# First stage of a four-layer conv network: sets formed by half a stack, one set of five summed on ScalarE, loads spread as three for two sets

## The chip, the cores and the metric

One core of a Trainium2 chip runs the whole program. The metric is device time in microseconds (us) of one launch. The kernel before takes 3494.92 us (median of 3 runs, 3491.64 to 3495.92).

The engines are TensorE (PE in the profile, its weight loads PEld), VectorE (DVE), ScalarE (ACT), GpSimd (POOL) and SyncE (SP). SP does nothing here but issue DMAs, in the order in which the program lists them.

## What is computed

The input x is 8 images of 384 channels of 32 x 32 pixels, fp32. Four layers follow one another, each `x = x + layer(groupnorm(x))`. The change touches the first layer alone, and of that the part up to the first q, k and v projections:

```python
def _gn(v, G=32, eps=1e-5):                 # mean and variance over 12 channels x 1024 pixels
    ...
def _dwproj(x, dw, g, b, pw):               # for each of q, k, v
    y = depthwise_conv_3x3(x, dw)           # 384 channels, padding 1
    y = gelu(_bn(y, g, b), approximate=False)   # mean and variance over batch and pixels
    return einsum('oc,bchw->bohw', pw, y)
q, k, v = (_dwproj(_gn(x), ...) for each)   # then softmax attention with 8 heads, w_out, _bn
```

The batch norm is what ties the stage together: no gelu of q can start before the depthwise convolution has run over all 8 images and its sums are known. The raw convolution results (q, k and v of 8 images, 36 MiB) [...] are written to DRAM and fetched back image by image in the attention stage.

## The kernel before

**Stacks.** The input is laid out on the host as 16 stacks of 1.5 MiB, `m = 4k + 2h + j`: image `2k + j`, half `h` of its channel groups. A stack is a tile of 128 partitions (32 row pairs of the picture, each with its two neighbour rows) by 6 slices of 512 values; the slices are `g * 3 + c`, with `g` in 0..1 a half of the stack and `c` in 0..2 the channel within a group of three. `load_tile` (L279) brings a stack in with four DMAs of 384 KB, one for each `d` (partitions `d::4`). The first four stacks go over SP and ACT, the next four over SP (L299 to L312).

**Units and sets.** The work list (L414) has 8 units `u = (k, h)`; unit u uses stacks 2u and 2u + 1. A unit has five sets in the order `y0 a1 y1 a2 v0` (unit 6 has no v set, unit 7 has the last two, `v-1 v0`), 40 sets in all, numbered n. A set is one group of matmuls on 32-row by 32- or 64-column tiles of TensorE (L574) that fills four PSUM banks:
- `y0` and `y1` make q, k and v of channel c = 0, for half g = 0 and g = 1
- `a1` and `a2` make q and k of channel c = 1 and c = 2, for both halves g
- `v0` makes v of channels 1 and 2 for both halves

So `a1`, the second set, already reads both halves of both stacks.

**After the matmuls** ScalarE copies the four banks to a tile `y` (L585; a pool of 4 tiles of 1 MiB, `ya`), VectorE takes the sums for the batch norm from `y` with four bn_stats (L591), and SP writes `y` to DRAM in four DMAs of 256 KB each, or two of 256 KB and two of 128 KB in a y set (L605). A `y` tile is free again when its writes have landed and its sums are taken.

**The group norm** of a unit, `norm(u)` (L339), is a list of ten steps: four `begin` (three bn_stats and an aggregate, L350 and L353, for each stack and half), `sums` (L366 to L379, the last on GpSimd), `spread` (L383 to L388), and four `apply` (ScalarE, L399; L397 on VectorE for the second stack of unit 0; then the two edge rows on GpSimd, L402). The table `steps` (L420) places the steps of unit u among the sets of units u - 2 and u - 1. `norm(0)` runs whole before the first set (L517).

**Order of DMAs.** All of this has one program order on every engine (a manual schedule). At set n SP gets, in this order: up to two pending loads (from n = 3 on, L534), then the four writes of the set. The pending loads are filled by unit (`LOADS`, L521): stacks 8 to 10 at unit 0, 11 and 12 at unit 1, 13 at unit 3, 14 and 15 at unit 4, and at unit 5 the raw v, k and q of image 0, fetched back in 18 DMAs of 256 KB (`fetch_raw`, L221). At the start of unit 7 (n = 34) eight small DMAs move the group norm's sums (`x_moments`, L508). GpSimd issues the loads of the weights (`load_late`, L319) at n = 0.

**The end of the stage.** Before the matmuls of n = 38 `spread_qk` (L427) gathers the q and k sums across partitions with two small matmuls (L442) and makes scale and shift (L497). After n = 38 ScalarE runs the gelu of q of image 0, after n = 39 that of k; then PE starts the projections `pq_first` (L258) and the attention stage.

Of the kernel before, what the change touches and what calls it, by code (L numbers as in the profile page):

```python
# [7 lines left out]
F32 = mybir.dt.float32  # L8
# [47 lines left out]
def tile_kernel(ctx: ExitStack, tc: tile.TileContext, i: dict, out: bass.AP):  # L56
# [210 lines left out]
    with ExitStack() as pa:  # L267
# [11 lines left out]
        def load_tile(m, queue):  # L279

            k, h, j = m // 4, m // 2 % 2, m % 2
            t = (
                image(f"xs{m}") if m in IN_IM
                else xa.tile([P, KC, N], F32, tag="xs", name=f"xs{m}")
            )
            xs_of[m] = t.rearrange("p c n -> p (c n)").rearrange("p (k n) -> p k n", n=HALF)

            def part(d):
                w = KC * N
                s = W + (0 if d in (1, 2) else W if d == 3 else -W)  # L290
                src = i["xs"][s : s + B * C * N].rearrange("(b e m n) -> b e m n", b=B, e=2, m=32)
                queue[d].dma_start(
                    out=t.rearrange("p c n -> p (c n)")[d::4],
                    in_=src[2 * k + j, 1 - d % 2, :, h * w : (h + 1) * w],
                )

            return [lambda d=d: part(d) for d in range(4)]

        for m in range(4):  # L299
            for f in load_tile(m, (nc.sync, nc.sync, nc.scalar, nc.scalar)):  # L300
                f()
# [13 lines left out]
        sels = wa.tile([P, 2, P], F32, name="sels_sb")  # L315
        isv = wa.tile([P, 7], F32, name="isv_sb")
        msk = wa.tile([P, 24], F32, name="msk_sb")
# [9 lines left out]
        xnst = wa.tile([P, B, KC, 2, 6], F32, name="xnst")  # L327
        sy = wa.tile([P, 16, NK, 6], F32, name="sy")
        sqk = wa.tile([P, KC - 1, 2, 4, NK, 6], F32, name="sqk")
        sv = wa.tile([P, 2, 4, NK, 6], F32, name="sv")  # L330
        zy = wa.tile([P, 16, 2], F32, name="zy")
        zqk = wa.tile([P, KC - 1, 8, 2], F32, name="zqk")
        zv = wa.tile([P, 8, 2], F32, name="zv")
        fqk = wa.tile([P, 2, 2, KC], F32, name="fqk")
        fv = wa.tile([P, 2, KC], F32, name="fv")
        room = wa.tile([P, 2, 160], F32, name="room")
        fs = wa.tile([P, 16], F32, name="fs")

        def norm(u):  # L339

            k, h = divmod(u, 2)
            mv = mvs[u % 2]
            turned = sa.tile([P, 2, 32], F32, tag="gp_t", name=f"gt{u}")
            rows = sa.tile([P, 2, 2, 16], F32, tag="gp_r", name=f"gr{u}")
            ss = sa.tile([P, 2, 32], F32, tag="gp_ss", name=f"gss{u}")
            small_ = sa.tile([P, 40], F32, tag="gp_s", name=f"gs{u}")

# [67 lines left out]
        for u in range(NU0):  # L415
            order = "y0 a1 y1 a2" + " v0" * (u < NU0 - 2) + " v-1 v0" * (u == NU0 - 1)
            work += [(u, w[0], int(w[1:])) for w in order.split()]
# [9 lines left out]
        def spread_qk():  # L427

            zs, nv, ng = (zy, zqk.rearrange("p c g s -> p (c g) s")), (3, 2), 16
            at = [slice(0, 96), slice(96, 160)]  # L430
            both = [
                room[:, 0, d].rearrange("p (v s g) -> p v s g", v=n, s=2)
                for d, n in zip(at, nv)
            ]
            v0 = 0
            for z, n, dst in zip(zs, nv, both):
                masked(z, n, v0, dst)
                v0 += n
            yield
            pm = big("pmove")  # L440
            for t, d in enumerate(at):
                nc.tensor.matmul(  # L442
                    pm[:, d], lhsT=sels[:, t, :], rhs=room[:, 0, d], start=True, stop=True,
                )
            got = room[:, 1, :96].rearrange("p (x g) -> p x g", g=16)
            nc.vector.tensor_tensor(
                got, pm[:, :96].rearrange("p (x g) -> p x g", g=16),
                msk[:, :16].unsqueeze(1).to_broadcast([P, 6, 16]), ALU.mult,
            )
            fy = fs[:, :6].rearrange("p (v s) -> p v s", v=3)  # L450
            nc.vector.reduce_sum(fy.rearrange("p v s -> p (v s)"), got, AX.X)
            got = room[:, 1, 96:].rearrange("p (x g) -> p x g", g=8)
            nc.vector.tensor_tensor(
                got, pm[:, 96:160].rearrange("p (x g) -> p x g", g=8),
                msk[:, 16:24].unsqueeze(1).to_broadcast([P, 8, 8]), ALU.mult,
            )
            f = fs[:, 8:16]
            nc.vector.reduce_sum(f, got, AX.X)
            nc.vector.tensor_copy(
                fqk[:, :, :, 1:], f.rearrange("p (v s c) -> p v s c", v=2, s=2)  # L460
            )
            nc.vector.tensor_copy(fqk[:, :, :, 0], fy[:, :2])
            nc.vector.tensor_copy(fv[:, :, 0], fy[:, 2])
            for v in range(2):
                scale_of(v, fqk[:, v])

        def masked(z, n, v0, dst):

            ng = z.shape[1]
            sq = sa.tile([P, ng], F32, tag="ssq", name=f"ssq{v0}")  # L470
            nc.vector.tensor_tensor(sq, z[:, :, 0], z[:, :, 0], ALU.mult)
            nc.vector.tensor_tensor(z[:, :, 1], z[:, :, 1], sq, ALU.add)
            for s in range(2):
# [5 lines left out]
        def spread_v():  # L479

            both = sa.tile([P, 32], F32, tag="bothv", name="bothv")
            masked(zv, 2, 5, both.rearrange("p (c s g) -> p c s g", c=2, s=2))
            yield
# [32 lines left out]

        for f in norm(0):  # L517
            f()
        quads = [slice(32 * r, 32 * r + 32) for r in range(4)]
        loads, norms_of = [], {}  # L520
        LOADS = {0: (8, 9, 10), 1: (11, 12), 3: (13,), 4: (14, 15)}  # L521
        for n, (u, kind, s) in enumerate(work):
            k, h = divmod(u, 2)
            at = n - first[u]
            if at == 0:
                for m in LOADS.get(u, ()):
                    loads += load_tile(m, 4 * (nc.sync,))
                if u == 0:
                    load_late()
                if u == 5:  # L530
                    acts[0] = {v: image(f"g{v}_0") for v in (2, 1, 0)}
                    for v, t in acts[0].items():
                        loads += fetch_raw(t, v, rqk[0], rv[:, 0])
            for _ in range(2):  # L534
                if loads and n > 2:
                    loads.pop(0)()
            if u == NU0 - 1 and at == 0:
# [15 lines left out]
            if kind == "v":  # L553
                h, c = h + s, 0
            else:
                c = s if kind == "a" else 0
            passes = [(j, x) for j in range(2 if kind == "v" else 1) for x in (1, 0, 2)]
            nq = 2 if kind == "y" else 4
            cols = [slice(P // nq * q, P // nq * (q + 1)) for q in range(nq)]
            for p in passes:  # L560
                j, x = p
                c0, c1 = max(0, 1 - x), W - max(0, x - 1)
                for q in range(nq):
# [3 lines left out]
                    elif kind == "y":  # L567
                        g, j, w = s, q, slice(0, 64)
                    else:
                        (g, j), w = divmod(q, 2), slice(0, 32)  # L570
                    src = xs_of[4 * k + 2 * h + j][:, g * KC + c, :]
# [11 lines left out]
            y = ya.tile([P, 4, HALF], F32, tag="y", name=f"y{n}")  # L583
            for src, r, w in outs:
                nc.scalar.copy(y[:, r : r + w, :].rearrange("p a n -> p (a n)"), src)  # L585
            st = (
                sy[:, 8 * h + 4 * s : 8 * h + 4 * s + 4] if kind == "y"
                else sv[:, h] if kind == "v" else sqk[:, s - 1, h]
            )
            for r in range(4):  # L590
                nc.vector.bn_stats(st[:, r, k, :], y[:, r, :])  # L591
            for q in range(4):
# [8 lines left out]
                else:  # L601
                    g, j = divmod(q, 2)
                    to = rqk[2 * k + j, s]
                g = 4 * (2 * h + g)
                nc.sync.dma_start(out=to[:, g : g + 4, :], in_=y[rows])  # L605
            if k == last:
                for r in range(4):
                    nc.vector.bn_aggr(
                        zy[:, 8 * h + 4 * s + r, :] if kind == "y"
                        else zv[:, 4 * h + r, :] if kind == "v" else zqk[:, s - 1, 4 * h + r, :],  # L610
                        st[:, r].rearrange("p a b -> p (a b)"),
                    )
            if n == len(work) - 2:
                gelu_image(acts[0][0], 0)
        assert not loads
        gelu_image(acts[0][1], 1)
# [1430 lines left out]
def _layouts(a):  # L2047
# [19 lines left out]
    for r in range(4):  # L2067
        for d in range(4):
# [11 lines left out]
        [  # L2080
            (own & (row % 64 < 48)).astype(f) / f(4),
            (own & (row // 64 == part // 32 % 2)).astype(f) / f(4),
# [3 lines left out]
        [  # L2086
            row // 16 % 4 == np.arange(3), row // 16 % 2 == np.arange(2),
            row // 32 % 2 == np.arange(2),
# [84 lines left out]
```

## Time and profile before

| what | value |
|---|---|
| runs of the kernel before | 3491.64, 3494.92, 3495.92 us |
| the profiled execution's own time | 3494.72 us |
| its span, first to last instruction | 3492.9 us |
| first matmul of the stage | 24.79 us after the span's start |
| first write of a `y` tile | 31.90 us |
| last write of the stage issued | 231.78 us |
| first projection `pq_first` on PE | 221.68 us |
| PE busy in the whole span | 3384.1 us (97%) |

The profile gives for each engine the time in which it was busy, and for each idle stretch what ended it (`<-ACT y` means that the instruction waited last for ScalarE's write of y). A queue's own lines (SPq) show the DMA issues: the time of an issue is how long the queue was held by it, not how long the transfer took. A table by windows shows busy time of each engine in us, the granted clock of TensorE, the mean busy share of the 16 DMA engines and the rate in GB/s. In the first 300 us the DMA engines move 78.38 MB, most of it in the first stage.

### The profile page before, as it was taken

The page shows a single profiled execution, that of the slowest core. Times are in us where ns is not written, and L with a number is a line of the kernel's source. Part 1 is how long each engine was busy: PE and PEld are TensorE (multiplying, and loading weights), DVE is VectorE, ACT ScalarE, POOL GpSimd, SP SyncE. Part 2 cuts the span into 40 slices and gives each one's busy share as a digit, 9 for nine tenths or more (in the row PEclk, how much of TensorE's full clock was granted, in tenths as well). Part 3 has the DMA queues.
Part 4 walks back from the last instruction along what each step waited for, and adds up shares of the span by engine and source line. Part 5 has one row for each costly group of instructions (what it writes and reads, how often), then busy time and mean ns, then how long its engine had stood idle before and what let it go on. Part 6 is the DMA issues. An engine that isn't in the chain of part 4 may idle for free.

```text
span 3492.9 us, 44919 instructions
## 1 busy us (share of the span) xinstructions
PE 3384.1 (97%) x18599; PEld 1458.3 (42%) x18599; DVE 1696.7 (49%) x2881; ACT 1298.5 (37%) x1514; POOL 206.1 (6%) x231
## 2 busy tenths in 40 slices
PE   6999999999999999998999999999999999999888
PEld 2333434343434343443344445344453444534434
DVE  8942232323232323234366365663656637566573
ACT  5655544444444444433222323313233232232222
POOL 2100000000000000000000200102001020010112
PEclk9999999999999999999999999999999999999898
DMA  9972121212121212123500101101111011110000
GB/s 357 295 205 79 26 79 27 79 26 79 26 79 26 79 27 78 28 79 125 220 24 21 50 39 35 40 21 50 40 35 40 21 50 40 35 39 18 0 37 19
DMA packets 86259, 234.01 MB, mean 67 GB/s; under 512 B 21672, under 2 KB 21896, under 8 KB 79130
## 3 DMA queue, kind: packets, MB, share of 16 engines
q1 hardware_dynamic: 83882, 222.75, 19.9%
q10 hardware_dynamic: 1248, 4.72, 0.3%
q8 instruction: 150, 2.46, 0.3%
q0 software_dynamic: 912, 3.53, 0.3%
q14 instruction: 67, 0.55, 0.1%
HBM read 145.77 MB, written 75.59 MB: 63 GB/s over the span
## 4 chain that ended last, share of the span: by engine, by line
PE 41%; DVE 9%; DMA 1%; ACT 1%; POOL 0%; issue 0%; DVEq 0%; ACTq 0%; POOLq 0%; SPq 0%
PE y L1502 12%; PE ph L1481 10%; DVE y L1577 5%; PE pq L1622 4%; PE pw L1585 3%; PE pf L1929 3%; PE s L1800 2%; PE pav L1826 2%; DVE hd L1467 1%; DMA o<-o 1%; PE pk L1775 1%; PE pv L1784 1%; PE xsb L1761 1%; PE pss L1839 1%; PE plog L1231 1%; DVE off L1692 1%
## 5 line engine op out<-in xcount | busy, mean ns | idle before, releaser
L827 ACT ACTIVATE p<-s 128x1024 f32<-128x1024 f32 x512 | 496.3, 1021 | 365.7 <-PE s L820 365.5
L835 PE MATMUL pav<-p,vt 64*64 64x512 f32 x4096 | 494.7, 588 | 0.0
L1481 PE MATMUL ph<-h,w_sb 128*128 128x512 f32 x1104 | 486.8, 595 | 6.3 <-ACT h L1430 6.3
L1502 PE MATMUL y<-hd,w_sb 128*128 128x512 f32 x1080 | 488.7, 600 | 3.5 <-DVE hd L1467 3.5
L820 PE MATMUL s<-qk,qk 48*64 48x512 f32 x2944 | 355.1, 592 | 0.0
L1481 PEld LDWEIGHTS ph<-h,w_sb 128*128 128x128 f32 x1104 | 207.0, 190 | 267.5 <-issue 249.8
L1502 PEld LDWEIGHTS y<-hd,w_sb 128*128 128x128 f32 x1080 | 199.9, 191 | 248.2 <-issue 235.8
L835 PEld LDWEIGHTS pav<-p,vt 64*64 64x64 f32 x4096 | 168.2, 133 | 273.7 <-issue 273.4
L796 DVE COPY ta<-pav 128x512 f32<-128x512 f32 (+1 forms) x65 | 44.2, 682 | 475.5 <-PE pav L835 475.5
L1491 ACT ACTIVATE hd<-ph,b_sb 128x512 f32<-128x512 f32 x180 | 122.7, 682 | 312.7 <-PE ph L1481 312.7
L1577 DVE SCALAR_TENSOR_TENSOR y<-h,tap,y 128x961 f32<-128x961 f32 (+1 forms) x192 | 233.8, 1241 | 0.6
L574 PE MATMUL pk<-xs,cws_sb 32*32 32x496 f32 (+3 forms) x3840 | 179.4, 601 | 39.4 <-DMA xs<-in_xs_dram 24.8
L1692 DVE SCALAR_TENSOR_TENSOR off<-q,dw_sb,off 128x225 f32<-128x225 f32 (+3 forms) x432 | 211.9, 544 | 1.6
L820 PEld LDWEIGHTS s<-qk,qk 48*64 48x64 f32 x2944 | 109.1, 133 | 211.4 <-issue 190.5
L1817 ACT ACTIVATE p<-s 128x1024 f32<-128x1024 f32 x96 | 96.1, 1023 | 166.5 <-PE s L1800 141.7
L81 DVE COPY qk<-pq 128x512 f32<-128x512 f32 x46 | 31.8, 691 | 251.9 <-PE pq L258 251.9
L1467 DVE TENSOR_TENSOR hd<-hd,cb 128x512 f32<-128x512 f32 x180 | 122.3, 684 | 41.0 <-ACT hd L1491 40.8
L574 PEld LDWEIGHTS pk<-xs,cws_sb 32*32 32x32 f32 (+1 forms) x3840 | 77.7, 111 | 139.4 <-issue 54.0
L1585 PE MATMUL pw<-y,upw 128*128 128x512 f32 x288 | 129.0, 601 | 4.9 <-DVE y L1577 4.9
L1862 POOL TENSOR_TENSOR p<-p,p 128x1024 f32<-128x1024 f32 x48 | 113.0, 2355 | 349.3 <-ACT p L1817 349.3
L820 PE MATMUL s<-ql,ql 48*64 48x512 f32 x1024 | 128.3, 592 | 0.2 <-ACT p L827 0.2
L1929 PE MATMUL pf<-att,wp_sb 128*128 128x512 f32 x288 | 127.6, 598 | 0.5 <-DVE x L1937 0.5
(326 smaller groups left out, 3718.1 us busy)
## 6 DMA issues: line engine op xcount, KB each, us to landing
rqk<-y SPq DMA_DIRECT2D x96, 256.0 KB
g<-rqk SPq DMA_DIRECT2D x96, 256.0 KB
xs<-in_xs_dram SPq DMA_DIRECT2D x56, 384.0 KB
g<-rv SPq DMA_DIRECT2D x48, 256.0 KB
xh<-in_x_dram SPq DMA_DIRECT2D x48, 256.0 KB
f<-in_x_dram SPq DMA_DIRECT2D x24, 512.0 KB
f<-o SPq DMA_DIRECT2D x24, 512.0 KB
o<-ot SPq DMA_DIRECT2D x42, 256.0 KB
```

What stands on the lines that cost most here:

```text
L574: nc.tensor.matmul(banks[r][cols[q]].rearrange("p (h w) -> p h w", w=W)[:, :, c0:c1], lhsT=cws[rs, c, 2 * h + g, x, w], rhs=src[rs, :, c0 ...
L820: nc.tensor.matmul(s[64 * k : 64 * k + 64, j * HALF : (j + 1) * HALF], lhsT=kt[r, k0 : k0 + 64], rhs=qt[r, h * HALF : (h + 1) * HALF], sta ...
L827: nc.scalar.activation(p, s, AF.Exp, scale=scale)
L835: nc.tensor.matmul(pav[k][64 * j : 64 * j + 64, :], lhsT=vts[b % 2][r, kc, 2 * hd : 2 * hd + 2, :].rearrange("p a b -> p (a b)"), rhs=p[r, ...
L1467: nc.vector.tensor_tensor(hd, hd, state["cb"], ALU.mult)
L1481: nc.tensor.matmul(ph, lhsT=w1[:, e, c, dc * P : (dc + 1) * P], rhs=state["h1"][c], start=(c == 0), stop=(c == KC - 1),)
L1502: nc.tensor.matmul(y, lhsT=w2[:, e, dc, m * P : (m + 1) * P], rhs=state[h, k], start=(k == 0), stop=(k == NE * KC - 1),)
L1577: nc.vector.scalar_tensor_tensor(d, f, tap2[:, c, t : t + 1], d, ALU.mult, ALU.add)
L1585: nc.tensor.matmul(pw[h], lhsT=upw2[:, c, m * P : (m + 1) * P], rhs=y[c][:, hs], start=(c == 0), stop=(c == KC - 1),)
L1622: nc.tensor.matmul(pq[h], lhsT=wq3[:, c, m * P : (m + 1) * P], rhs=h3[h][:, c, :], start=(c == 0), stop=(c == KC - 1),)
L1692: nc.vector.scalar_tensor_tensor(d, f, dw3[:, t : t + 1], d, ALU.mult, ALU.add)
L1929: nc.tensor.matmul(pf[:, hs], lhsT=wp3[:, pr, m * P : (m + 1) * P], rhs=att[:, pr, hs], start=(pr == 0), stop=(pr == NPAIR3 - 1),)
```

## The change

Four things are changed in the first stage; the arithmetic is otherwise the same.

1. **Halves at the start.** Stacks 0 and 1 are loaded as halves g (8 DMAs of 192 KB each instead of 4 of 384 KB), first both first halves, then both second ones. `norm(0)` is run twice, once for each half: its `sums` and `spread` run twice.
2. **Sets by half.** The order in a unit becomes `y0 a0 y1 a1 v0`: an a set now makes channels c = 1 and 2 of one half g. `y0 a0` read the first halves only. The destination of its four writes becomes channel 1 of both images, then channel 2 of both, at one half; it was both images at the first half, then at the second.
3. **ScalarE sums one set of five.** In `y1`, ScalarE does four Identity activations from PSUM to `y` and four Square activations in place in PSUM, each with an accumulated sum, and the four bn_stats on VectorE are gone.
4. **Loads at an even rate.** One load before even sets, two before odd ones, from n = 1 on, from one list: stacks 8 to 12, raw v of image 0, stacks 13 to 15, raw k, raw q. It is used up at n = 33.

With these goes a different layout of the sums in `spread_qk`: one matmul over 224 columns instead of two over 96 and 64, one multiply and one reduction instead of two each, and one copy more.

```diff
-        for m in range(4):
-            for f in load_tile(m, (nc.sync, nc.sync, nc.scalar, nc.scalar)):
+        both = (nc.sync, nc.sync, nc.scalar, nc.scalar)
+        halves = [load_tile(m, both) for m in range(2)]
+        for g in range(2):
+            for m in range(2):
+                for f in halves[m][4 * g : 4 * g + 4]:
+                    f()
+        for m in range(2, 4):
+            for f in load_tile(m, both):
                 f()
...
-            order = "y0 a1 y1 a2" + " v0" * (u < NU0 - 2) + " v-1 v0" * (u == NU0 - 1)
+            order = "y0 a0 y1 a1" + " v0" * (u < NU0 - 2) + " v-1 v0" * (u == NU0 - 1)
...
-        for f in norm(0):
-            f()
+        for g in range(2):
+            f = norm(0, g)
+            for t in (g, 2 + g, 4, 5, 6 + 2 * g, 7 + 2 * g):
+                f[t]()
...
-        LOADS = {0: (8, 9, 10), 1: (11, 12), 3: (13,), 4: (14, 15)}
+        def later():
+            for m in (8, 9, 10, 11, 12, 2, 13, 14, 15, 1, 0):
+                if m > 2:
+                    parts = load_tile(m, 4 * (nc.sync,))
+                else:
+                    t = acts[0][m] = image(f"g{m}_0")
+                    parts = fetch_raw(t, m, rqk[0], rv[:, 0])
+                for f in parts:
+                    yield f()
...
-            for _ in range(2):
-                if loads and n > 2:
-                    loads.pop(0)()
+            for _ in range(1 + n % 2 if n else 0):
+                next(loads, None)
...
-                        (g, j), w = divmod(q, 2), slice(0, 32)
+                        (c, j), w = divmod(q, 2), slice(0, 32)
+                        g, c = s, c + 1
...
+            on_act = kind == "y" and s == 1
+            if on_act:
+                for r in range(4):
+                    nc.scalar.activation(
+                        y[:, r, :], banks[r], AF.Identity, accum_out=sums1[:, h, r, k, 0:1]
+                    )
+                for r in range(4):
+                    nc.scalar.activation(
+                        banks[r], banks[r], AF.Square, accum_out=sums1[:, h, r, k, 1:2]
+                    )
+            else:
+                for src, r, w in outs:
+                    nc.scalar.copy(y[:, r : r + w, :].rearrange("p a n -> p (a n)"), src)
+                for r in range(4):
+                    nc.vector.bn_stats(st[:, r, k, :], y[:, r, :])
...
-                    g, j = divmod(q, 2)
-                    to = rqk[2 * k + j, s]
+                    c, j = divmod(q, 2)
+                    g, to = s, rqk[2 * k + j, 1 + c]
...
+                if on_act:
+                    nc.vector.reduce_sum(z, sums1[:, h].rearrange("p r k s -> p r s k"), AX.X)
+                    nc.vector.tensor_scalar(z, z, 1.0 / (NK * HALF), None, ALU.mult)
```

## The prediction

> **What bounds the kernel now.** The slices of the page first (40 of 87 us each):
>
> ```profile
> PE   6999999999999999998999999999999999999888
> DVE  8942232323232323234366365663656637566573
> DMA  9972121212121212123500101101111011110000
> ```
>
> PE is at 9 tenths or more from the second slice almost to the end, and at 6 in the first, where DVE and DMA are high. So only the first stage is open, and behind it the attention stage runs at PE's pace: what the stage loses or gains passes to the end one for one. Next, the busy time by windows inside the stage (core time, then PE, PEld, DVE, ACT, POOL, clock, DMA share, GB/s):
>
> ```profile
> 60.00:80.00 20.00, 18.06 (x453) 8.69 (x429) 18.99 (x41) 14.12 (x18) 3.31 (x9) 1.00 0.92 315
> 80.00:100.00 20.00, 18.81 (x449) 8.45 (x449) 19.69 (x41) 13.30 (x15) 2.61 (x8) 1.00 0.96 326
> 180.00:200.00 20.00, 16.82 (x239) 5.02 (x222) 9.80 (x28) 12.32 (x15) 2.26 (x7) 0.91 0.87 281
> ```
>
> Two things are full: DVE (19.69 of 20 us) and the DMA engines (0.92 to 0.96). From 180 us DVE is half idle and the stage goes no faster. To see which one leads, I put the timeline's ScalarE copies beside SP's writes of the same set. First the copies of sets n = 12 (a y1) and n = 14 (a v0) with their first writes, then the end of the stage:
>
> ```profile
> 83.77 2.05 ACT L585 COPY y<-pk 128x512 f32<-128x512 f32 x4 [0.27 <-DMA rqk<-y]
> 94.23 2.05 ACT L585 COPY y<-pk 128x512 f32<-128x512 f32 x4 [1.65 <-DMA rv<-y]
> 98.11 0.99 SPq L605 DMA_DIRECT2D rqk<-y  x2
> 104.89 4.01 SPq L605 DMA_DIRECT2D rv<-y  x4
> ...
> 204.60 6.96 SPq L512 DMA_DIRECT2D xnst<-xst  x8
> 211.66 1.04 SPq L605 DMA_DIRECT2D rqk<-y  x2
> 217.02 2.05 ACT L585 COPY y<-pk 128x512 f32<-128x512 f32 x4 [7.30 <-DMA rv<-y]
> 219.09 1.28 ACT L243 ACT_TABLE_LOAD   x1
> 221.68 5.96 PE L258 MATMUL pq_first<-g,wq_sb 128*128 128x512 f32 x12
> ```
>
> Set 12 is in SBUF at 83.77 + 2.05 = 85.82, and SP issues its first write at 98.11: 12.3 us later. For set 14 it is 104.89 - 96.28 = 8.6. I counted this lag for all 40 sets: 0.0, 1.8 and 1.2 us for n = 0 to 2, then 3.2 or more, 7 to 12 from n = 7 on, 17 at n = 34. It is never used up. SP's queue is one unbroken stream from 31.90 to 233.0 us: 160 writes, 32 loads, 18 fetches, 8 moves of sums = 218 issues in 201.1 us, 0.92 each. **The stage is bound by SP's DMA stream**, and the last lines show how it reaches the end: set 38's copy waits until set 34's write lands, that write stands behind everything else in SP's queue, and the gelu of q and `pq_first` follow at once.
>
> By units (first write of y0 to the next unit's), SP takes 26.9, 23.9, 21.9, 26.1, 26.5 us for units 1 to 5, with 10, 6, 4, 8 and 10 loads or fetches in them. DVE (first L591 to the next unit's) takes 22.8, 22.7, 23.1, 23.1, 25.2. DVE is full, but it is the slower one only in unit 3, and there a backlog of 7 us or more still stands in SP's queue.
>
> [...] Every write here leaves from 32 or 16 partitions; [...] 409 to 430 GB/s at a share of 1.0 while loads run (10 to 45 us), 265 GB/s at 0.95 while only writes run (225 to 230 us). The change alters neither. [...] no run shows Square here.
>
> **The change part by part.** All sums against the profiled execution, 3494.72 us (span 3492.9; the median of runs is 0.2 above it).
>
> *Halves at the start.* Removed: the wait for all of two stacks (first bn_stats 9.85 us, second stack 14.88). Half of each is 1.5 MiB, what stack 0 was, so both are there near 10 us. Then DVE: one more begin 2.1, sums 1.6, POOL 0.72, spread 0.7: near 15; ACT's first apply is near 16, since ACT first issues 12 loads at the DMA rate, then a table load of 1.28. Apply 1.6 and edges 0.7 give a first matmul near 18.5, 6 us ahead of 24.79. But DVE does sums and spread twice (3.2 us more) and so comes to unit 1's begins (L350) at about 24.7, against 24.15 now; and, above all, SP issues loads of stacks 4 to 7 until 30.45 (29.98 + 0.47), and set 0's write is behind them. It can start at 30.5 instead of 31.90: **-1.45 us**. POOL issues `load_late` (9 DMAs, 6.1 us) after the second half's edges, at about 26, as now (26.66); the rsqrt of unit 1 behind them was at 34.04 and stays. The 8 more issues lie under a saturated stretch (share 1.0): 0. Beyond the 1.45, SP's waits put down to ScalarE's y are 4.6 us in all; the other 3.15 fall where lags were only 1 to 2 us, but reads filled the engines (share 1.0 to 45 us). Bounds 0 and -3.15; I take **-1.0**.
>
> *Sets by half.* Same matmuls, same bytes. PE's waits for POOL's xs after the first 24.8 us (14.7 + 6.4 us over the stage) shrink; PE isn't last, so 0. What was late behind it is SP. The a sets' destinations change; SP's own time for four writes without loads before them is 3.2 to 3.8 us in a sets, 3.75 to 4.1 in v sets, whose order alternates between channels. Bounds: -0 and 16 x 0.5 = +8; I take 0[...].
>
> *ScalarE sums y1.* Four L591 in a row take 2.41 to 2.47 us; DVE loses 2.44 in 8 sets; per unit 22.8 becomes 20.4. Hidden behind SP: 0; if SP were not there, up to 6 x 2.44 = 14.6 (units 6 and 7 have no DVE load). ACT's 4 copies (2.05) become 8 activations. No row shows such an activation with a sum, so I bound one by L585's 0.51 (back to back) and L1430's 0.81 (128x512), and take 0.68 (L1491, from PSUM): 5.4 us, +3.4. ACT has per unit 4 applies x 1.69 and 5 copies x 2.0 = 16.8; with it 20.2, under SP's 22 to 27. Table loads for Square: 0, or 2 x 1.28 per y1. Queued behind the Squares are the next apply and a1's copies; PE needs the banks two sets later (about 10 us); SP's writes wait for the Identities alone, with 7 us of stock. Only at n = 36 can it show: copies there at 201.96, so sums to 207.4, while set 37's copy starts at 207.79 when set 33 lands: cover 0.4. With the bound of 0.81 it costs 0.7. I take 0.
>
> *Even loads.* The same 50 loads all stand ahead of set 34's write: 0 in total. A pair of loads adds 1.80 us to a y set, 1.55 to an a set, 2.3 to a v set; alone at the head one takes 0.93. So grouping matters by at most 0.1 per load; 16 sets get a single one: +-1.6, I take 0. No load stalls SP: stack 11 at n = 9 needs unit 0's tiles (done at n = 4), stack 13 at n = 18 unit 2's, stack 14 at n = 21 unit 3's (n = 19, and PE is two sets ahead of SP); raw v at n = 14 needs set 9's write landed, issued 18 us before.
>
> *spread_qk.* One matmul pair less, wider columns, one copy (0.16) more: 0 within 0.3.
>
> Sum: 3494.72 - 1.45 - 1.0 = **3492.3 us**. Late next is what is late now: SP's stream.
>
> **Rivals.** *DVE leads in the units where it is full.* For: 19.69 of 20 us. Against: the lag. Then 6 x 2.44 + 1.45 = 16 us off: 3478.7; half of it, if SP limits half the units: 3486. *The head start passes through.* For: set 0 starts 6 us earlier, and at n = 0 to 2 SP is nearly starved. Against: SP is busy with loads to 30.45 and the engines are full. 4.6 to 7 us off: 3488 to 3490, at most. *The new write order is slower.* Place: L605 in 16 a sets, channel 1 then channel 2, each 8 KB slab apart from its neighbour, where now two writes fill adjoining slabs. If an a set then takes a v set's 4.05 instead of 3.55: +8, and the stream carries it all: 3494.7 - 2.4 + 8 = 3500.3. It decides from 2.4 / 16 = 0.15 us per set on. *The change doesn't do what it says*, with the head start eaten by DVE's second sums: 3494.7, within the forecast's case.
>
> **How the numbers follow.** Forecast with its neighbours (SP leads, 3488 to 3499, head start included): 0.63. DVE leads wholly or by half (3478 to 3487): 0.24. Slower writes, or ScalarE late by table loads: 0.13. A measurement tells about 0.2% (7 us) from no change: faster 0.25, same 0.62, slower 0.13. The range leaves out the full DVE case and the slower end: 3481 to 3499.
>
> **What would show it.** Right: first matmul near 18.5; first write near 30.5; DVE at 17 to 18 of 20 us while DMA stays at 0.92 to 0.96; lags of 5 us and more; last write near 229; `pq_first` near 219. Wrong: lags that fall to zero or `pq_first` before 214 (DVE led), four writes of an a set over 4 us (write order), ScalarE with table loads in the stage.

## The result and the profile after

| | before | after |
|---|---|---|
| median of 22 runs each | 3491.89 us | 3497.81 us |
| lowest to highest | 3488.05 to 3496.92 | 3493.52 to 3502.33 |
| ratio, with its 95% interval | | 1.0016 (1.0009 to 1.0022) |
| the profiled execution, its span | 3494.72, 3492.9 us | 3500.56, 3498.8 us |
| first matmul | 24.79 | 19.15 us |
| SP's loads of stacks 0 to 7 issued | 30.45 | 33.03 us |
| first write of y | 31.90 | 33.98 us |
| `pq_first` | 221.68 | 229.92 us |
| first exp of attention | 238.65 | 246.89 us |

The change is slower, by 5.9 us; the forecast was 2.4 faster. Two profiles of the same kernel before differ by 3.4 us at the stage's end (`pq_first` at 221.68 and at 225.11), so below it is the medians that carry the verdicts; a profile only shows where to look.

The slices of the page after. DVE has fallen in the first two digits (8 and 9 to 7 and 7), PE in the second (9 to 8), and a PE slice in the middle of the program, where attention ends, has gone from 8 to 7:

```profile
PE   6899999999999999997999999999999999999888
DVE  7752232323232323234266375663756637566563
DMA  9972121212121212023600111101101011110000
```

The windows of the stage (busy us of PE, PEld, DVE, ACT, POOL, then clock, DMA share, GB/s), first one from before, then those after:

```profile
10.00:20.00 10.00, 0.00 (x0) 0.00 (x0) 8.82 (x20) 1.28 (x1) 0.00 (x0) 1.00 1.02 430
```

```profile
10.00:20.00 10.00, 0.85 (x8) 0.54 (x16) 7.72 (x21) 2.95 (x2) 1.98 (x5) 1.00 0.96 370
...
60.00:80.00 20.00, 17.62 (x421) 7.54 (x416) 16.57 (x32) 16.85 (x31) 2.97 (x9) 1.00 0.93 292
80.00:100.00 20.00, 17.21 (x401) 8.08 (x388) 16.69 (x38) 14.77 (x27) 2.96 (x9) 0.91 0.91 299
180.00:200.00 20.00, 16.21 (x296) 6.18 (x288) 13.79 (x39) 16.65 (x29) 2.64 (x7) 0.86 0.90 277
```

DVE has the relief it was to have (18.99 to 16.57, 19.69 to 16.69), ScalarE carries it (14.12 to 16.85), and the DMA rate is no higher than before (315 and 326 GB/s there). Two things are new: from 10 to 20 us the engines move 370 GB/s instead of 430, and PE's clock is 0.91 and 0.86 where it was 1.00 and 0.91. The timeline, with sets 0 and 14 and then the end:

```profile
26.22 3.85 ACT L610 COPY y<-pk 128x512 f32<-128x512 f32 x6
33.98 1.37 SPq L626 DMA_DIRECT2D rqk<-y  x2
...
100.31 2.05 ACT L610 COPY y<-pk 128x512 f32<-128x512 f32 x4 [2.77 <-PE pk L586]
110.34 3.90 SPq L626 DMA_DIRECT2D rv<-y  x4
...
211.94 6.84 SPq L516 DMA_DIRECT2D xnst<-xst  x8
218.88 1.05 SPq L626 DMA_DIRECT2D rqk<-y  x2
225.26 2.06 ACT L610 COPY y<-pk 128x512 f32<-128x512 f32 x4 [8.00 <-DMA rv<-y]
229.92 5.97 PE L258 MATMUL pq_first<-g,wq_sb 128*128 128x512 f32 x12
```

Set 0 is in SBUF at 28.25 (26.22 and four of the six copies), yet its write starts at 33.98: the head start stands in SP's queue for 5.7 us. Set 14 waits 8.0 us (110.34 - 102.36). This lag of the write behind the copies is 2.2 us or more at every set. So PE's new pauses, seen in the waits of the stage (total us, times, longest), are not what ends last:

```profile
PEld pk L586 <- ACT pk L605: 39.5, 25, 9.6
PE pk L586 <- ACT pk L605: 23.5, 8, 8.8
```

### The profile page after: what moved, and what is told of

Its sections match the earlier page's. It is cut to its first block, busy times and chain, and to the rows that moved or that the text cites. A ratio compares the mean times of both kernels' runs of the same rounds, so it can differ in the third digit from the quotient of the medians.

```text
span 3498.8 us, 45021 instructions
## 1 busy us (share of the span) xinstructions
PE 3382.2 (97%) x18597; PEld 1456.9 (42%) x18597; DVE 1680.1 (48%) x2854; ACT 1320.8 (38%) x1616; POOL 206.6 (6%) x232
## 4 chain that ended last, share of the span: by engine, by line
PE 41%; DVE 9%; ACT 1%; DMA 1%; POOL 1%; issue 0%; DVEq 0%; ACTq 0%; POOLq 0%
PE y L1524 12%; PE ph L1503 9%; DVE y L1599 5%; PE pq L1644 4%; PE pw L1607 3%; PE pf L1951 3%; PE s L1822 2%; PE pav L1848 2%; DVE hd L1489 1%; DMA o<-o 1%; PE pk L1797 1%; PE pv L1806 1%; PE xsb L1783 1%; PE plog L1253 1%; PE pss L1861 1%; DVE off L1714 1%
```

## The experiments

All kernels were timed in five rounds against the kernel before on the same chip. The kernel before against itself tells what this can resolve:

> The kernel before once more, unchanged, for a second profile and for what the comparison gives where nothing differs: within 0.05% of before, the first projection at 220 to 223 us.

Measured 3492.2, ratio 1.0 (0.9991 to 1.0008): about 3 us either way. The first projection came at 225.11, later than the 220 to 223 expected.

### One part of the change undone at a time

`e1_pairs`: the changed kernel with the old grouping of loads.

```diff
-            for _ in range(1 + n % 2 if n else 0):
-                next(loads, None)
+            for _ in range(2):
+                if loads and n > 2:
+                    loads.pop(0)()
```

> The changed kernel with the loads again in pairs from n = 3 on, filled by units as before; all else as changed. Theory of the grouping (a load that comes alone costs SP's stream 1.05 to 1.1 us, one of a pair 0.9; 16 sets have one alone): 3 us faster than the changed kernel, so about 3 us slower than the kernel before. Rival, write order or ScalarE's sums carry the loss: as the changed kernel, 6 us slower than before.

Measured 3498.16, ratio 1.0017 (1.0009 to 1.0026), as the change: the grouping is worth nothing that this comparison could see.

`e2_whole`: stacks 0 and 1 in whole DMAs, unit 0's norm once; all else as in the change.

```diff
-            if m < 2:
-                return [... for g in range(2) for d in range(4)]
...
-        for g in range(2):
-            f = norm(0, g)
-            ...
+        for f in norm(0):
+            f()
```

> The changed kernel with stacks 0 and 1 loaded whole and the first norm run once, all else as changed. Theory of the start (DMAs of half the size keep fewer bytes in flight, and SP's first write starts 2.1 us later): 2 us faster than the changed kernel, 4 us slower than before. Rival, the head start of PE is worth something: slower than the changed kernel by up to 6 us.

Measured 3494.74, ratio 1.0005 (0.9996 to 1.0013): 3.1 us of the 5.9 go with the halves. By the profiles, 2.4 of these lie far behind the stage (below), so 0.7 is left for the start itself.

`e3_dve_sums`: all sums on DVE. Besides what the expectation says, y0's and y1's sums then share one place, so the norms aren't the reference's.

```diff
-            on_act = kind == "y" and s == 1
+            on_act = False
```

> The changed kernel with the sums of y1 on VectorE again (four bn_stats after four copies). Theory that SP's stream leads: within 1.5 us of the changed kernel, 5 to 7 us slower than before, with VectorE back near 19 of 20 us. Rival, the longer hold of PSUM by ScalarE costs: 3 to 5 us faster than the changed kernel. Rival, VectorE's relief was worth something: slower than the changed kernel by 3 us and more.

Measured 3496.58, ratio 1.0009 (1.0000 to 1.0017). `e4_order_only` has both edits and the old grouping of loads, so that only sets by half and the layout of the sums are left of the change:

> Only the sets by half, with their write order and the other layout of the sums; loads, start and sums as before. Theory of the write order (two neighbouring slabs no longer written one after the other): 3 to 6 us slower than before. Theory that the loss lies in start and grouping: within 1.5 us of before.

Measured 3494.82, ratio 1.0006 (0.9997 to 1.0014). Against `e2_whole` (3494.74), ScalarE's sums cost nothing; halves at the start without them (`e3_dve_sums` against this one, which differ in the grouping of loads too) cost 1.8.

`e11_halves_alone` puts the halves alone into the kernel before (the first and second hunk of the change, and the norm of unit 0 in two parts), `e12_sets_only` the order of sets alone:

```diff
-            order = "y0 a1 y1 a2" + ...
+            order = "y0 a0 y1 a1" + ...
...
-                        (g, j), w = divmod(q, 2), slice(0, 32)
+                        (c, j), w = divmod(q, 2), slice(0, 32)
+                        g, c = s, c + 1
...
-                    g, j = divmod(q, 2)
-                    to = rqk[2 * k + j, s]
+                    c, j = divmod(q, 2)
+                    g, to = s, rqk[2 * k + j, 1 + c]
```

> The kernel before with the halves of the first two stacks alone (16 DMAs of half the size, norms of unit 0 in two parts); sets, sums and loads as before, so the second set still needs both halves. Theory A (the half-size loads keep fewer bytes under way, SP's loads end 2 to 2.6 us later and the stream starts that much later): first matmul 19 to 25 us, SP's loads end near 33 instead of 30.5, first write near 33.5 instead of 31.9, time +1.5 to +2.6: 3494 to 3495. Theory B (the head start is worth something by itself and is lost to the other parts of the change): first write by 30.5, time -1 to -2.5: 3490 to 3491.5.

Measured 3494.58, ratio 1.0003 (0.9995 to 1.0011). First matmul at 19.84, SP's loads issued at 33.93, first write at 34.86: the start behaves as in the change without any of its other parts.

> The kernel before with the order of sets alone (each set of q and k takes one half of the rows of both channels); loads, start and the layout of the sums are as before, so the sums of the two channels of q and k are mixed and the norms of these are not the reference's. Theory A (the order by half costs the 2.3 us that were found with the start whole and DVE's sums): 3494 to 3495. Theory B (the layout of the sums and the wider spread at the stage's end cost them): 3492.5, as before.

Measured 3493.51, ratio 1.0002 (0.9994 to 1.0010). It lies between the two theories; order and layout together (`e4_order_only`) cost 2.4 by the medians, with no cost at all still inside the interval, and these runs can't divide them.

### The rival that the prediction priced highest: the write order

`e7_dest_scattered` gives the kernel before the new destinations, `e8_dest_adjacent` the change the old ones:

```diff
-                    to = rqk[2 * k + j, s]
+                    g, to = s - 1, rqk[2 * k + j, 1 + g]
...
-                    g, to = s, rqk[2 * k + j, 1 + c]
+                    g, to = c, rqk[2 * k + j, 1 + s]
```

> The kernel before with one thing changed: the destinations of the four writes of an a set, which go to four separate slabs of 8 KB per row (two channels, two images) as in the changed kernel, instead of two pairs of adjoining slabs. q and k of channels 1 and 2 are then stored in exchanged places. Theory of the write order: an a set's writes take about 0.4 us longer, the first projection starts 4 to 7 us later and the kernel is 3 to 6 us slower. Rival, the loss with the order of the sets comes from elsewhere: within 1.5 us of before.

> The changed kernel with the destinations of an a set's writes as before (two pairs of adjoining slabs), which stores q and k of channels 1 and 2 in exchanged places; all else as changed. Theory of the write order: 3 to 6 us faster than the changed kernel, which leaves it 0 to 3 us slower than before (the start). Rival: as the changed kernel, 6 us slower than before.

Measured 3491.26, ratio 0.9994 (0.9986 to 1.0002), and 3496.83, ratio 1.0011 (1.0004 to 1.0017). Scattered destinations don't slow the kernel before, adjacent ones don't cure the change (1.0 us, within noise). In the traces the four writes of an a set hold SP for 3.6 us on average before and after (sets from n = 5 on). This rival falls.

### Two microseconds far behind the stage

The marks of the stage's end don't hold all of the loss. From attention's last exp to the gate's matmul `plog` it is 30.9 us after and 28.5 before. A run-time branch lies there. DVE's first instruction behind it, in the change and in `e2_whole` (in brackets the idle time and what ended it):

```profile
1643.72 0.17 DVE L1208 TENSOR_REDUCE gws<-gw_sb 128x4 f32<-128x12 f32 x1 [5.87 <-issue]
```

```profile
1639.31 0.07 DVE L1201 MEMSET pres<- 128x8 f32 x1 [3.59 <-DVEq L1025]
```

The change, `e1_pairs` and `e8_dest_adjacent` idle 5.5 to 5.9 us, all others 3.6 to 3.9. `e10_dve_shift` moves DVE's stream on by 26 instructions:

```diff
+        idle = wa.tile([P, 2], F32, name="idle")
+        for _ in range(26):
+            nc.vector.memset(idle, 0.0)
```

> The changed kernel with 26 memsets of 128x2 on DVE ahead of everything, where DVE waits for the first stack: nothing in the stage changes, but all later DVE instructions stand 26 places further on in DVE's stream. Theory A (about 2.2 us of the loss lie after the run-time branch behind attention, where DVE is idle 5.5 to 5.9 us in the three kernels with halves at the start and sums on ScalarE, and 3.6 in all others; this comes from where DVE's instructions stand, not from the stage): DVE is idle 3.6 us there, from the end of attention to the gate matmul 28.5 us instead of 30.9, and the time falls by about 2.2, to 3495.5. Theory B (that idle time goes with the work of the stage): 5.9 us again and 3497.8.

```profile
1636.75 0.17 DVE L1211 TENSOR_REDUCE gws<-gw_sb 128x4 f32<-128x12 f32 x1 [3.63 <-DVEq L1033]
```

Measured 3495.48, ratio 1.0005 (0.9997 to 1.0013): the idle time is back at 3.63, 28.5 us to the gate, 2.3 us less than the change.

Other traces confirm that it is the place in the stream. Count DVE's records from the first one, its waits included. In the change, `e1_pairs` and `e8_dest_adjacent`, DVE pauses 1.9 to 2.1 us behind record 1402, between two waits just behind the branch. In the change with loads on POOL (`e13_after_pool`, below) three records fewer stand ahead of the branch, and the pause, 1.31 us, comes behind record 1403. In `e2_whole` 14 fewer stand ahead of it, and what is left is 0.18 us, behind record 1402:

```profile
1637.30 0.36 DVE L1237 TENSOR_TENSOR gate<-gw_sb,rs 128x28 f32<-128x28 f32 x3 [1.31 <-POOL gate L1224]
```

```profile
1641.17 0.26 DVE L1232 TENSOR_TENSOR gate<-gw_sb,rs 128x28 f32<-128x28 f32 x2 [0.18 <-issue]
```

(The first line puts its pause down to a memset of GpSimd, but that memset had ended 1.35 us earlier.) In all five kernels the record behind the pause starts 2.3 to 2.5 us after the first one behind the branch, so the further behind the branch it stands, the less shows. In the kernel before and in `e10_dve_shift` this place lies ahead of the branch, and there is no pause. What waits there stays open: no trace shows it.

### What bounds the stage: SP's queue or the engines behind it

`e5_moments_late` puts the eight moves of x's sums behind the last write, so that set 34's write doesn't stand behind them:

```diff
-            if u == NU0 - 1 and at == 0:
-                x_moments()
...
+        x_moments()
         gelu_image(acts[0][1], 1)
```

> The kernel before with the eight small moves of the group norm's sums taken out of SP's queue at n = 34 and put behind the last write of the stage. Theory that SP's stream leads the stage: set 34's write comes 7 us earlier, the first projection starts 5 to 7 us earlier and the kernel is 4 to 7 us faster than before. Rival, VectorE or PE leads at the end of the stage: within 1.5 us of before.

Measured 3492.21, ratio 0.9995 (0.9987 to 1.0004). In its profile `pq_first` comes at 219.57, but that one execution (3484.42) is the fastest of its 13; the median shows nothing. The 4 to 7 us of the theory didn't come: what stands ahead of set 34's write is not by itself what sets the end of the stage. `e6_pool_loads` takes the 32 loads of stacks 8 to 15 off SP, in the kernel before:

```diff
-                    loads += load_tile(m, 4 * (nc.sync,))
+                    loads += load_tile(m, 4 * (nc.gpsimd,))
```

> The kernel before with the 32 loads of stacks 8 to 15 issued on POOL's queue instead of SP's; the same bytes, the same order of sets. Theory A (what is full is the 16 DMA engines, at 0.92 to 0.96, and SP's time per issue is only their pace): no gain, 3489 to 3496, SP's own writes grow from 0.92 to over 1.0 us each while the loads run beside them. Theory B (SP's queue as such limits, 0.92 us for each issue): 32 x 0.92 = 29 us less in SP's stream, DVE with 22.8 us a unit is next, so 10 to 15 us faster: 3478 to 3483.

Measured **3480.34**, ratio 0.9963 (0.9951 to 0.9975). The windows of the kernel before from 40 to 60 us, and of this one from 40 to 100:

```profile
40.00:60.00 20.00, 18.00 (x402) 7.23 (x413) 19.55 (x43) 14.19 (x18) 2.65 (x7) 1.00 0.93 343
```

```profile
40.00:60.00 20.00, 17.61 (x398) 6.90 (x410) 19.34 (x43) 13.79 (x17) 6.94 (x16) 1.00 1.01 404
60.00:80.00 20.00, 18.71 (x453) 8.43 (x427) 19.62 (x42) 14.66 (x18) 7.51 (x17) 1.00 0.99 393
80.00:100.00 20.00, 17.24 (x419) 7.29 (x419) 18.27 (x35) 13.85 (x17) 4.75 (x13) 1.00 0.96 318
```

Same bytes, but the engines go from 0.93 and 0.92 to 1.01 and 0.99: they had not been full, SP's queue held them back. The issuer's queue was the stage's bound, and relieving it was worth 12.4 us of the 29 taken out of it (an estimate: 32 issues of 0.92 us). DVE as the next limit, which theory B assumed, is not confirmed below.

### The change with SP's queue relieved

If SP's queue hid the relief of DVE, it should show now. Four kernels, all with loads on POOL: the change; the change with whole stacks at the start; that with all sums on DVE (again y0's and y1's in one place); and the second with the moves of x's sums on POOL too. The first edit is in all four, the second in the last:

```diff
-                    parts = load_tile(m, 4 * (nc.sync,))
+                    parts = load_tile(m, 4 * (nc.gpsimd,))
...
-                    nc.sync.dma_start(
+                    nc.gpsimd.dma_start(
                         out=xnst...
```

> The changed kernel with the loads of stacks 8 to 15 on POOL's queue. Theory A (SP's queue led and hid the relief of DVE; with SP relieved, as in the kernel before with POOL's loads at 3480.3, DVE with 19.3 to 19.6 of 20 us and the DMA engines at 0.93 on average from 40 to 200 us are next, so taking 2.44 us a unit from DVE pays up to the engines' limit, 0.065 x 160 = 10 us): 3470 to 3477. Theory B (the change's own 5 us of loss stay whatever leads): 3483 to 3486.

> The same with stacks 0 and 1 loaded whole and unit 0's norm in one part: sets by half, sums on ScalarE, loads on POOL. Against the kernel with the halves: theory A of the start (half-size loads end later and cost 2 to 3 us): 2 to 3 us faster than that one. Rival (with SP relieved the earlier first matmul pays): 2 to 5 us slower than that one.

> The last one with all sums on DVE (the square of the mean isn't added to the sums of the fifth that ScalarE took): only the order of sets, the layout of the sums and the grouping of loads differ from the kernel before with POOL's loads at 3480.3. Theory A (DVE leads once SP is relieved): 5 to 10 us slower than with ScalarE's sums, near 3480 to 3483. Theory B (the DMA engines lead then): within 2 us of it.

> Sets by half, sums on ScalarE, whole stacks at the start, loads on POOL, and the 8 moves of x's sums on POOL's queue too, which is idle from 185 to 206 us in the kernel before with POOL's loads, where they hold SP for 7.0 us ahead of set 34's write. Theory A (SP still leads at the end of the stage): up to 5 us faster than with the moves on SP. Theory B (at the end the writes' bytes lead, as moving them behind the last write gave 0.3 us with the loads on SP): within 1.5 us of it.

| kernel | median us | ratio (95%) |
|---|---|---|
| `e13_after_pool` | 3493.79 | 1.0003 (0.9994 to 1.0011) |
| `e14_whole_pool` | 3490.46 | 0.9992 (0.9983 to 1.0000) |
| `e15_whole_pool_dve` | 3480.46 | 0.9965 (0.9953 to 0.9977) |
| `e16_moments_pool` | 3490.19 | 0.9993 (0.9984 to 1.0001) |

The first two theories of `e13_after_pool` both miss: it is slower than either said. The last row shows that moving x's sums off SP too brings nothing. Halves cost 3.3 (first two rows), of which 1.3 by the profiles is the pause behind the branch; order and layout cost nothing (3480.46 against 3480.34), and **ScalarE's sums cost 10.0 us** (second and third row): not relief but a load. Waits and two windows of `e14_whole_pool`, then the same windows of `e15_whole_pool_dve`:

```profile
PEld pk L581 <- ACT pk L600: 30.7, 25, 3.9
PE pk L581 <- ACT pk L600: 14.9, 7, 3.1
```

```profile
60.00:80.00 20.00, 17.69 (x378) 7.47 (x368) 15.26 (x30) 16.82 (x30) 5.75 (x14) 0.91 0.92 327
100.00:120.00 20.00, 16.94 (x372) 6.83 (x370) 15.64 (x37) 16.44 (x32) 3.31 (x9) 0.91 0.90 257
```

```profile
60.00:80.00 20.00, 17.29 (x432) 7.59 (x432) 17.69 (x36) 13.72 (x16) 4.62 (x12) 1.00 0.98 370
100.00:120.00 20.00, 18.18 (x433) 7.29 (x431) 19.56 (x44) 13.67 (x17) 4.72 (x11) 1.00 0.93 293
```

PE does 372 matmuls where it did 433, at a clock of 0.91, and SP waits 22.9 us for ScalarE's y in the stage (6.4 in the other). The lag of the writes behind the copies tells the same. Its median over the 40 sets is 9.7 us before and 9.3 in the change, 3.8 in `e15_whole_pool_dve`, and 0.4 in `e14_whole_pool`, where 18 sets are written within 0.3 us: there SP's queue has run dry, and ScalarE is what it waits for. In `e15_whole_pool_dve` a stock is still there, 5 us or more from n = 26 to 37. The change itself shows how a Square holds a bank, at the first y1:

```profile
38.87 1.67 ACT L408 ACTIVATE xs<-xs,gss 128x1536 f32<-128x1536 f32 x1 [8.80 <-DVE gss L397]
40.45 0.57 ACT L601 ACTIVATE y<-pk 128x512 f32<-128x512 f32 x1
40.92 0.19 ACT L601 ACTIVATION_READ_ACCUMULATOR y<-pk 128x1 f32 x1
...
42.73 0.61 ACT L605 ACTIVATE pk<-pk 128x512 f32<-128x512 f32 x1
43.50 7.09 PE L586 MATMUL pk<-xs,cws_sb 32*32 32x512 f32 x126 [8.76 <-ACT pk L605]
```

PE stands from 34.74 until a Square (L605), which reads the bank in PSUM, lets it go. The Squares make up only the last 2.3 us of these 8.76, from the end of the first Identity (41.02) to the end of the first Square (43.34); before that ScalarE itself had stood 8.80 us for DVE's part of the next norm (gss). Later pauses for a Square are 2.1 to 3.5 us. PE's clock is 0.50 from 37.4 us, in the midst of this pause of 8.76 us, to 47.6. Two last kernels separate hold from work: `e17_squares_sbuf` lets the Squares read y in SBUF, `e18_fifth_unsummed` leaves the fifth's sums out.

```diff
-                        banks[r], banks[r], AF.Square, accum_out=sums1[:, h, r, k, 1:2]
+                        sqs, y[:, r, :], AF.Square, accum_out=sums1[:, h, r, k, 1:2]
...
-                for r in range(4):
+                for r in range(0 if kind == "y" and s == 1 else 4):
                     nc.vector.bn_stats(st[:, r, k, :], y[:, r, :])
```

> The kernel with whole stacks at the start, sums on ScalarE and loads on POOL (3490.5), but with ScalarE's Squares reading y in SBUF and writing to a scratch tile there, so that PE's banks come free after the Identities; ScalarE's work stays the same. Theory A (what made ScalarE's sums cost 10 us once SP was relieved is that the Squares keep the PSUM banks 2.5 us longer, PE stands still and its clock falls to 0.50 for some us in each unit): PE's waits for ScalarE's sums go, the clock stays at 1.00 to 180 us, and the time falls by 6 us or more, to 3475 to 3484. Theory B (it is ScalarE's own time, 2.7 us more a unit, which comes late with the next apply and copies): within 3 us of 3490.5.

> Sets by half, whole stacks at the start, loads on POOL, all sums on DVE (3480.5), but the sums of the fifth of the sets that the change gives to ScalarE left out altogether, so the norms aren't the reference's: DVE is relieved by 2.44 us a unit at no cost to any other engine. Theory A (with SP relieved DVE leads): 5 to 12 us faster, 3468 to 3475. Theory B (the DMA engines, 0.93 to 1.02 busy, or ScalarE and PE lead then): within 3 us of 3480.5.

Measured 3483.46, ratio 0.9981 (0.9972 to 0.9990), and 3481.45, ratio 0.9971 (0.9962 to 0.9981). So the hold is a half or more of the 10.0: 7.0 us as medians, 4.9 when each kernel is set against the kernel before on its own chip (7.3 and 2.4 faster). PE has no wait for the Squares left and its clock is 1.00 in all windows up to 180 us but one:

```profile
60.00:80.00 20.00, 16.80 (x360) 7.15 (x344) 13.20 (x25) 15.68 (x27) 4.14 (x11) 0.91 0.95 349
100.00:120.00 20.00, 17.02 (x438) 7.12 (x422) 17.02 (x40) 16.29 (x31) 4.22 (x10) 1.00 0.95 281
```

The rest fits ScalarE's own time, as SP still waits 18.6 us for its y, but no run separates it. And relieving DVE at no cost to anyone (3481.45 against 3480.46) brings nothing with SP relieved either. As a stock still stands before SP there (median lag 4.5 us), this doesn't tell what DVE is worth where SP never leads. None of these beats `e6_pool_loads`, one word changed in the kernel before, which beats both kernels.

## Why the prediction was wrong, point by point

**What bounds: right, but for the end of the stage.** Lags above 2 us at every set after the change too, and 12.4 us for taking loads off SP. It was not seen that the stream could be widened, as the engines were at 0.92. The path at the end, by which set 34's write is late because of all that stands ahead of it, is not confirmed: without the eight moves ahead of it the median is 0.3 us lower (`e5_moments_late`). The reading "7 to 12 from n = 7 on" leaves out 14.2 and 13.7 us at n = 35 and 36 and the fall to 3.5 at n = 39; nothing rests on it.

**Halves at the start: the step that failed.** "It can start at 30.5 instead of 31.90: -1.45 us", and -1.0 of SP's waits. The first matmul came as said (18.5 forecast, 19.15 measured), but the first write came at 33.98, because SP's loads ended 2.6 us later and not at the same time. "The 8 more issues lie under a saturated stretch (share 1.0): 0" was the error: with DMAs of half the size the engines moved 370 GB/s from 10 to 20 us, where they had moved 430.

The records of the trace show why. SP and ACT use eight completion semaphores in turn for their DMAs (numbers 100, 102 and 111 to 116, before and after), and an issue waits until the DMA that last used its semaphore has landed. So at most eight DMAs of the two are under way: 3.1 MB of 384 KB each, 1.6 MB of 192 KB. This wait is what paces the start: of SP's issues of this kind up to 33.5 us, 18 of 22 before and 19 of 24 after begin within 0.06 us of that landing (from then to 235 us before, 7 of 218). By 10 us SP's and ACT's loads had moved 2.13 MB before and 1.65 after, while GpSimd's first loads, which have semaphores of their own, had moved 0.64 and 1.28. By 20 us GpSimd's stood at 1.48 in both, the others at 5.59 and 5.15: 0.44 MB less, 1.0 us at the 427 GB/s of the next 10 us. What the rest of the 2.6 is wasn't settled, and no run changes the number of eight.

Measured alone, the step is +1.8 instead of -2.45 (interval -1.8 to +3.8). Three other pairs of kernels give 0.7, 1.8 and 2.0, without the pause behind the branch: each within noise, all of one sign.

**Sets by half: 0, the author's estimate, within its bounds** (0 to +8), but not by write order; +0.8 alone, +2.4 with the layout of sums, 0.1 with loads on POOL, none of them clear of noise.

**ScalarE's sums: 0, right for the wrong reason.** 4.8 us a set (40.45 to 45.25) against 5.4 forecast, and no table load. But "PE needs the banks two sets later (about 10 us)" was wrong: PE waited for Squares 8 times, 8.8 us at most, 2.3 of it for the Squares themselves. It cost nothing only because SP's stock of finished sets covered it; with that cover thinner it costs 10.

**Even loads: 0, right** (`e1_pairs`). The spread was not tested apart from the order of sets. **DVE as leader: right to reject**: its relief brings nothing even with 32 loads off SP's queue (`e18_fifth_unsummed`).

**Not foreseen:** some 2.2 us behind attention, which come from DVE's place in its stream and which no reading of the stage could show. Halves 1.8, order and layout 0.8 to 2.4, and these 2.2 make 4.8 to 6.4; measured 5.9. Each of the three alone is within what one comparison can't tell from zero; their sum isn't.

## What to carry to other kernels

If an engine's DMA queue is one unbroken stream and the engines stand at 0.92, try a second issuing queue before relieving any compute engine: here one word was worth 12.4 us, and the relief of a DVE that was 98% busy nothing. A head start is worth what the first waiting queue can use of it: here set 0 stood in SP's queue for 5.7 us. Cutting loads in halves can slow that very queue: here at most eight DMAs were under way, and the engines moved 370 GB/s from 10 to 20 us where they had moved 430. So look which wait each issue ends. The Squares that moved to ScalarE and read PSUM held a bank 2.3 us longer at the first y1, and letting them read SBUF was worth 7.0 us as medians: with such work, ask when PE wants that bank back.

## What was not expected of the hardware

- An activation with an accumulated sum (128x512, L601 and L605 of the change) is two instructions: 0.57 to 0.61 us and a read of the accumulator of 0.19 to 0.22, which overlap (0.57 to 0.60 us a pair, back to back).
- SP and ACT together had at most eight DMAs under way. That is a limit of the program's semaphores and not shown to be one of the queue. In the middle of the stage it was the issues themselves that held SP: a write of y took 0.81 us on average before and 0.84 after, with the engines at 0.92 to 0.96 and 0.91 to 0.93 from 60 to 140 us.
- Behind a run-time branch DVE idled 5.87 us in the change and 3.63 with 26 memsets more ahead of it in its stream (`e10_dve_shift`): in five kernels the record behind place 1402 or 1403 started 2.3 to 2.5 us after the first one behind the branch.
